# Cross-attention on one core: the step order of the last tiles, the PSUM banks of the score columns, and the operands of the vector norm

## The chip, the cores and the metric

The kernel runs on one core of a Trainium2 chip. The engines of the core are TensorE (PE, matmuls; PEld is its weight load), VectorE (DVE), ScalarE (ACT), GpSimd (POOL) and SyncE (SP, which issues all DMAs here). Each works through its own instructions in order. The working memory is SBUF; matmuls write to PSUM, which has eight banks of 128 partitions by 512 floats. The metric is device time in microseconds (us) of one execution.

## The reference

Four sequences of 2048 rows of x (512 wide) attend to four contexts of 77 rows (384 wide), everything in float32. Cut to what is computed:

```python
text_p  = x @ W_text + b_text
audio_p = ctx @ W_audio + b_audio
Q = layer_norm(text_p, g1, beta1)
K = layer_norm(audio_p, g2, beta2)
alpha = softmax(Q @ K.T / sqrt(512))
h = (alpha @ audio_p) @ W_out + b_out
out = layer_norm(h + x, g_out, beta_out)
```

## The kernel before, in words

The projection of x is never formed. The kernel computes, once for each sequence, a matrix M with which x gives the unscaled scores directly, and vw, the context's values already multiplied by W_out. The variance of a projected row, which the first layer norm needs, is a quadratic form of x; U holds its (upper triangular) matrix in four column chunks. M and U stand side by side in `mu` (two buffers, one for each parity of the sequence); U's last chunk stands in `ub`.

The 8192 rows of x are 64 tiles of 128 rows. Four tiles are a group, which is one load of x (`load_x`, five buffers) and four of a second, spread copy xq (`spread_x`, two buffers). The steps of a tile have one-letter names in the code:

- x (`turn`, L378): DVE turns the tile's xq into xt.
- p and P (`begin_project`, `end_project`, L427 and L435): PE multiplies xt by mu, chunk 3 and 2 in p, chunk 1 and 0 in P, into a bank y; the columns of U's last chunk go to another bank, yl. That is five matmuls a tile, and the profile shows two instructions for each float32 matmul.
- s and t (`score`, `score_rest`): DVE takes the 80 score columns out of y (L462) and sums the products of U's columns with x (L451), for y in s and for yl in t.
- r, c, e for a batch of tiles: POOL computes the row scale by a power (L477, L187), DVE scales the scores and takes the maximum (L484, L487), ACT takes the exponentials (L494).
- w and W (`turn_weights`, L506, L507): PE turns the weights of two tiles, ACT copies them to et.
- a (`apply`, L514): PE multiplies et by vw into a bank h. i, z (L520, L527): DVE inverts the sums and forms z = h/sum + x. q, d (L535, L543, L544, L187): ACT sums the squares, ACT and POOL make the mean and the inverse deviation of the second norm.
- The second norm goes one of two ways. o, y, m: DVE makes a shift (L566), ACT normalizes z (L571), POOL multiplies by g_out and adds beta_out (L575, L576). v (`norm_on_vector`, L558, L559): DVE does it in two instructions. In either way the tile is then stored (L551).

PSUM has eight banks: two for y, two for h, one for each of yl0 and yl1, prep and gain. yl of tile n is in bank yl0 or yl1 by the parity of n, and the turned weights (`et_ps`) use the other one. From slot 20 on, copies of the rows w (used by L484) and of g_out (`kept[1]`, in bank gain) stand in PSUM. The vector norm writes its intermediate zc into the y bank scored last, reads g_out from bank gain (from SBUF before slot 20), and beta_out from SBUF.

The order is the order in which the code is written: `in_program_order` ties each instruction to the one before on its engine. Two pieces of code issue the steps. For slots n = 0 to 39 a loop (L711 to L731) issues, with n the tile being projected: p of n, s and t of n-1, P of n, the norm of n-12, x of n+2, z of n-7, a of n-6, and at fixed slots of every four the batch's steps. The vector norm there is that of every fourth tile, and stands ahead of x and z of its slot. A list written out by hand (L734 to L761) holds all steps from tile 40 on; the batches there are of two tiles from tile 48 on and of one tile for 62 and 63 (`LAST`, L385). Copies of the next sequence's M into mu (L676, POOL) stand at slots 15, 20 and 36. In the list 13 tiles go the way of v (33, 36, 42, 43, 47, 50, 52, 55, 56, 58, 60, 62, 63), in the loop seven (3, 7, ... 27).

Of the kernel before, what the change touches and what calls it, by code (L numbers as in the profile page):

```python
# [29 lines left out]
P = 128  # L30
# [18 lines left out]
def tile_xattn(  # L49
# [40 lines left out]
    def bank(tag, name):  # L90
        return (ps2 if tag in ("h", "y") else ps1).tile([P, 4, P], F32, tag=tag, name=name)

# [85 lines left out]
    four = [flat(bank(tag, f"w_ps_{tag}_{i}")) for i, tag in enumerate(("y", "y", "yl0", "yl1"))]  # L178
# [22 lines left out]
    def prepare(batches, last_columns):  # L201
# [19 lines left out]
        def turned_rows(rows, src, tag):  # L221

            n = rows.stop - rows.start
            pt = bank("prep" if in_slots or tag == "vat" else "gain", f"{tag}_ps_{b0}_{rows.start}")
            for k in range(src.shape[1] // P):
                nc.tensor.transpose(
                    pt[:, k, :n], src[:n, k * P : (k + 1) * P], ident[:n, :n]
                )
            return pt[:, : src.shape[1] // P, :n]
# [155 lines left out]
    LAST = [2, 2, 2, 2, 2, 2, 2, 1, 1]  # L385
    batches, start = [], 0
    for size in [T] * ((NT - sum(LAST)) // T) + LAST:
        batches.append(range(start, start + size))
        start += size
    batch_of = {n: tiles for tiles in batches for n in tiles}  # L390

    ys, state, kept, scored_y = {}, {}, [], []
    begun = [-1]
# [25 lines left out]


    def project_chunks(n, ks):
        mub = made[groups[n // T][0]][0]
        xt = turned[n]
        y, b = ys[n]
        for k in ks:
            cols = slice(0, SQ + min(k + 1, LAST_K) * R)
            nc.tensor.matmul(  # L427
                parts(y[:, : Q * AQ])[:, :, cols],
                lhsT=xt[:, k, :],
                rhs=mub[:, k, :, cols],  # L430
                start=(k == LAST_K),
                stop=(k == 0),
            )
            if k == LAST_K:
                nc.tensor.matmul(  # L435
                    b, lhsT=xt[:, k, :], rhs=ub.rearrange("p q i -> p (q i)"), start=True, stop=True
                )

    def begin_project(n):

        begun[0] = n
        slot_begins(n)
        ys[n] = flat(bank("y", f"y_{n}")), flat(bank(f"yl{n % 2}", f"yl_{n}"))[:, :P]
        project_chunks(n, (3, 2))

    def end_project(n):
        project_chunks(n, (1, 0))
        del turned[n]

    def sum_of_products(y, x, first, to):  # L450
        nc.vector.tensor_tensor_reduce(  # L451
            out=y, in0=y, in1=x, scale=1.0, scalar=first, op0=ALU.mult, op1=ALU.add, accum_out=to
        )

    def score(n):

        i, t = divmod(n, T)
        scored_y[:] = ys[n][:1]
        y = parts(ys[n][0][:, : Q * AQ])
# [3 lines left out]
        xp = parts(xs[i][:, t, :])[:, :, : LAST_K * R]  # L463
        sum_of_products(y[:, :, SQ:], xp, e[:, S : S + 1], s.sa[:, c])

    def score_rest(n):

        i, t = divmod(n, T)
        s, c = of(n)
        yl = parts(ys.pop(n)[1])  # L470
        sum_of_products(yl, parts(xs[i][:, t, :])[:, :, LAST_K * R :], s.sa[:, c], s.ss[:, c])

    def row_scale(f):

        s = state[f]
# [4 lines left out]
    def scale_scores(f):  # L480
        s = state[f]
# [7 lines left out]
    def exponential(f):  # L489
        s = state[f]  # L490
# [5 lines left out]
    def turn_weights(f, a=0):  # L496


        s = state[f]
        z = a + min(s.m, 2) if s.m == T else s.m  # L500
        if a == 0:
            s.et = soft.tile([S, T, P], F32, name=f"et_{f}", tag="et")

        pe = bank(f"yl{(begun[0] + 1) % 2}", f"et_ps_{f}_{a}")
# [13 lines left out]
    def invert(f):  # L518
        s = state[f]
        nc.vector.reciprocal(s.inv[:, : s.m], s.inv[:, : s.m])  # L520

    def residual(n):

        i, t = divmod(n, T)
        s, c = of(n)
        z = s.z[n] = zs.tile([P, H], F32, name=f"z_{n}", tag="z")
# [12 lines left out]
    def deviations(f):  # L539

        s = state[f]
# [11 lines left out]
    def norm_on_vector(n):  # L553
        s, c = of(n)
        z = s.z[n]

        zc = scored_y[0]
        nc.vector.scalar_tensor_tensor(zc, z, s.nm[:, c], kept[1] if kept else go, ALU.add, ALU.mult)  # L558
        nc.vector.scalar_tensor_tensor(z, zc, s.ro[:, c], beo, ALU.mult, ALU.add)  # L559
        store(n)  # L560

    def norm_shift(f):

        s = state[f]
# [3 lines left out]
    def norm_on_scalar(n):  # L568
        s, c = of(n)
        z = s.z[n]  # L570
        nc.scalar.activation(z, z, AF.Identity, bias=s.no[:, c], scale=s.ro[:, c])  # L571

    def norm_on_gpsimd(n):
        z = of(n)[0].z[n]
        nc.gpsimd.tensor_tensor(z, z, go, ALU.mult)  # L575
        nc.gpsimd.tensor_tensor(z, z, beo, ALU.add)  # L576
        store(n)

# [76 lines left out]
    M_MOVED = 4  # L655
    KEPT = 20
    later_steps = prepare(list(range(1, B)), 0)

    def keep():

        kept.append(bank("prep", "w_ps"))
        for b in range(B):
            nc.scalar.copy(kept[0][:, b, :S], made[b][1][:, 1, :S])
        kept.append(flat(bank("gain", "gain_ps")))
        nc.scalar.copy(kept[1], go)

    def slot_begins(n):

        i, t = divmod(n, T)
        b, g = groups[i]  # L670
        if t == 0:
            load_x(i + 2)
        if t == 2:
            spread_x(i + 2)
        if b + 1 < B and n % (NG * T) == (M_MOVED if b else NG * T - 1):
            nc.gpsimd.tensor_copy(  # L676
                mu[(b + 1) % 2][:, :, :, :SQ], later[b + 1].rearrange("p k (q m) -> p k q m", q=Q)
            )

    do = dict(  # L680
        x=turn,
        p=begin_project,
        P=end_project,
        s=score,
        t=score_rest,
        r=row_scale,
        c=scale_scores,
        e=exponential,
        w=turn_weights,
        W=lambda f: turn_weights(f, T // 2),  # L690
        i=invert,
        a=apply,
        z=residual,
        q=squares,
        d=deviations,
        o=norm_shift,
        y=norm_on_scalar,
        m=norm_on_gpsimd,
        v=norm_on_vector,
    )  # L700

    def run(steps, n):

        for step, back in steps:
            if n - back >= 0:
                do[step](n - back)

    for n in range(40):  # L711
        t = n % T
        run([("p", 0), ("s", 1), ("t", 1), ("P", 0)], n)
        on_vector = t == T - 1
        if not on_vector:
            run([("o", 12)] * (t == 0) + [("y", 12)], n)
        if t == 0:
            run([("r", 4)], n)
        run([("v" if on_vector else "m", 12)], n)
        if n == KEPT:  # L720
            keep()
        else:
            next(steps if n < 2 else later_steps, None)
        run([("x", -2)], n)
        run([("i", 7)] * (t == 3) + [("z", 7)], n)
        if t == 0:
            run([("c", 4)], n)
        run([("a", 6)], n)
        run({1: [("w", 5)], 2: [("W", 6)]}.get(t, []), n)
        run([("q", 7)], n)  # L730
        run({0: [("e", 4)], 2: [("d", 10)]}.get(t, []), n)  # L731


    for step in """  # L734
        o28
        p40 s39 z33 y28 y29 a34 t39 a35 r36 z34 P40 c36
        p41 m29 s40 y31 x42 t40 P41 m31
        p42 z35 y30 P42 q33 q34 s41 q35 e36 t41 d32 w36 m28 x43
        p43 s42 P43 o32 t42 a36 y35 i36 v33 x44 y32 a37 s43
        p44 x46 m30 t43 W36 P44 r40 z36 z37 a39 m32 a38 x45 c40 s44 y34 z39  # L740
        p45 P45 t44 q37 z38 e40 x47
        p46 q36 s45 x48 q39 P46 m35 t45 q38 s46 w40 d36 i40 o36 m34 y38
        p47 P47 t46 W40 v36 a40 y37 s47 z40 a42 t47 a43 z42 x50 x49 a41 z41 z43 q42 q40 m38 y39
        p48 q41 r44 P48 c44 q43 m37 s48
        p49 d40 t48 e44 x51 w44 v43 P49 W44 a45 m39 a47 o40 s49
        p50 y41 i44 x52 t49 m41 z45 P50 z47 a46 q45 v42 z46 a44 y40 s50 q47 z44 x53 t50 r48 q46 m40
        p51 P51 c48 s51
        p52 t51 q44 d44 e48 o44 y45 x54 r50 i48 m45 P52 w48
        p53 P53 s52 a48 y46 c50 t52 e50 a49 x55 v47 m46 s53 y44 i50 z48 t53 w50
        p54 P54 x56 q48 z49 s54 a51 a50 z51 r52  # L750
        p55 z50 q49 m44 t54 c52 q51 x57 P55 q50 d48 d50 o48 s55 e52 i52 o50
        p56 t55 v50 y48 w52 P56 s56 a52 m48 r54 a53 y49
        p57 z52 m49 t56 y51 z53 c54 q52 P57 x58 q53 e54 w54
        p58 x59 a55 d52 s57 t57 o52 P58 v52 r56 i54 c56 y53 x60
        p59 s58 z55 t58 P59 e56 a54 w56 s59 i56 z54
        p60 t59 m53 P60 x61 m51 a57 r58 a56 q54 q55 x62 c58 s60 d54 o54 z57 e58 y54
        p61 z56 m54 t60 v55 q57 w58 P61 i58 q56 a59 d56 a58 s61 x63
        p62 t61 o56 y57 P62 z58 z59 r60 m57
        p63 q59 c60 s62 P63 e60 v56 q58 t62 s63 i60 d58 o58 w60 t63 a60 r62 c62 z60 a61 r63 y59 e62 w62 i62
        c63 e63 a62 q60 z61 i63 w63 z62 v58 a63 q61 q62 m59 z63 d60 o60 d62 v60 v62 q63 y61 d63 m61 v63  # L760
    """.split():  # L761
        do[step[0]](int(step[1:]))
# [36 lines left out]
```

## Time and profile before

| | us |
|---|---|
| median of 3 runs | 309.1 (308.82 to 309.45) |
| the profiled execution | 309.45 |
| its span, first to last instruction | 306.6 |
| 64 residuals z on DVE (L527) | 46.7 busy, 734 ns each |
| 64 transposes xt on DVE (L378) | 44.7 busy, 703 ns each |
| 20 vector norms on DVE, L558 and L559 | 15.3 and 15.0 busy |
| 44 norms on POOL, L575 and L576 | 56.0 and 56.2 busy, 1272 and 1277 ns each |
| 44 norms on ACT (L571) | 35.1 busy, 808 ns each |
| 64 second stages on PE (L514), 2 instructions each | 63.9 busy, 596 ns each |

The page has a line for each engine with its busy time, share of the span and number of instructions. The 40 slices show the busy share in equal parts of the span, in tenths. Engines work side by side, so busy times do not add up to the span; the chain of waits tells which of them the end waited for. Groups of instructions have mean durations; the timeline has single ones with their start.

### The profile page before, as it was taken

How to read it: one execution, taken by the hardware profiler on the slowest of the kernel's cores; microseconds unless marked ns; L12 is line 12 of the kernel's file. 1: busy time of each engine (PE TensorE's matmuls, PEld its weight loads, DVE VectorE, ACT ScalarE, POOL GpSimd, SP SyncE). 2: the span in 40 equal slices, each digit the busy share in tenths (PEclk: the TensorE clock that was granted, in tenths of full speed). 3: DMA queues.
4: the chain of work that ended last, by engine and by line, in shares of the span. 5: the costliest groups of instructions: out<-in, count | busy, mean ns of one | idle time of the engine just before them, and what ended most of it. 6: DMA issues, size and time to landing. Idle time of an engine off the chain costs nothing.

```text
span 306.6 us, 4110 instructions
## 1 busy us (share of the span) xinstructions
PE 291.1 (95%) x1096; PEld 177.2 (58%) x1096; DVE 241.3 (79%) x742; ACT 135.8 (44%) x398; POOL 163.2 (53%) x195
## 2 busy tenths in 40 slices
PE   8899999999999999989999999999999999999950
PEld 8568565566777556555555655655555565565520
DVE  3643368877855776998998989888989998999985
ACT  3241011063532243463654536374737656527471
POOL 0010002010552346656867585779888787876774
PEclk9999999999999999999999999999999999999995
DMA  7998792907418616819596969688896979320214
GB/s 237 234 368 260 200 214 97 250 20 138 138 38 168 205 54 157 245 70 253 197 271 175 279 152 285 146 266 166 297 225 207 237 243 202 112 101 34 105 53 186
DMA packets 54356, 55.85 MB, mean 182 GB/s; under 512 B 2531, under 2 KB 35619, under 8 KB 54333
## 3 DMA queue, kind: packets, MB, share of 16 engines
q1 hardware_dynamic: 54333, 55.59, 66.8%
q8 instruction: 8, 0.13, 0.2%
q14 instruction: 15, 0.12, 0.1%
HBM read 38.49 MB, written 16.78 MB: 180 GB/s over the span
## 4 chain that ended last, share of the span: by engine, by line
PE 84%; DVE 7%; DMA 4%; issue 1%; ACT 1%; SPq 1%; POOL 0%; ACTq 0%; DVEq 0%
PE y L427 46%; PE h L514 16%; PE yl L435 4%; PE vw_ps L235 3%; PE m_ps L305 3%; PE va_ps L235 3%; PE et_ps L506 2%; DMA wa<-in_L_xattn_W_audio_dram 2%; PE w_ps_yl L623 2%; DMA xq<-in_x_dram 2%; PE uw_ps L328 2%; DVE y L451 1%; DVE y L558 1%; DVE z L559 1%; PE w_ps_y L623 1%
## 5 line engine op out<-in xcount | busy, mean ns | idle before, releaser
L427 PE MATMUL y<-mu,xt 128*128 128x464 f32 (+2 forms) x512 | 179.0, 473 | 0.0
L427 PEld LDWEIGHTS y<-mu,xt 128*128 128x128 f32 x512 | 89.7, 190 | 49.4 <-issue 34.2
L575 POOL TENSOR_TENSOR z<-z,go 128x512 f32<-128x512 f32 x44 | 56.0, 1272 | 26.6 <-ACT z L571 26.4
L514 PE MATMUL h<-vw,et 77*128 77x512 f32 x128 | 63.9, 596 | 1.3 <-ACT et L507 1.2
L535 ACT ACTIVATE sqj<-z,sz 128x512 f32<-128x512 f32 x64 | 46.2, 722 | 38.1 <-DVE z L527 34.5
L576 POOL TENSOR_TENSOR z<-z,beo 128x512 f32<-128x512 f32 x44 | 56.2, 1277 | 3.4
L527 DVE SCALAR_TENSOR_TENSOR z<-h,inv,x 128x512 f32<-128x512 f32 x64 | 46.7, 734 | 4.8 <-PE h L514 3.4
L378 DVE STREAM_TRANSPOSE xt<-xq 128x512 f32<-128x512 f32 x64 | 44.7, 703 | 0.0
L451 DVE CUSTOM_DVE_ANT_1 y<-y,x,e 128x384 f32<-128x384 f32 x64 | 40.1, 626 | 2.3
L507 ACT COPY et<-et_ps 77x256 f32<-77x256 f32 (+1 forms) x33 | 11.9, 362 | 64.4 <-PE et_ps L506 64.4
L571 ACT ACTIVATE z<-z,no,ro 128x512 f32<-128x512 f32 x44 | 35.1, 808 | 10.9 <-DVE no L566 10.8
L435 PEld LDWEIGHTS yl<-ub,xt 128*128 128x128 f32 x128 | 23.5, 188 | 26.4 <-issue 13.0
L477 POOL TENSOR_SCALAR rs<-ss 128x4 f32<-128x4 f32 (+2 forms) x21 | 4.8, 227 | 51.2 <-DVE ss L451 31.2
L462 DVE TENSOR_TENSOR e<-y,uw 128x80 f32<-128x80 f32 x64 | 15.1, 236 | 20.6 <-PE y L427 20.4
L514 PEld LDWEIGHTS h<-vw,et 77*128 77x128 f32 x128 | 23.0, 190 | 11.7 <-issue 5.9
L494 ACT ACTIVATE e<-e,mx 128x77 f32<-128x77 f32 x64 | 22.3, 352 | 15.3 <-DVE mx L487 15.1
L451 DVE CUSTOM_DVE_ANT_1 yl<-yl,x,sa 128x128 f32<-128x128 f32 x64 | 22.7, 354 | 3.4
L435 PE MATMUL yl<-ub,xt 128*128 128x128 f32 x128 | 24.7, 274 | 0.0
L187 POOL TENSOR_TENSOR rs<-rs,mhalf 128x4 f32<-128x4 f32 (+2 forms) x21 | 18.6, 887 | 1.7
L187 POOL TENSOR_TENSOR ro<-ro,mhalf 128x4 f32<-128x4 f32 (+2 forms) x21 | 18.3, 871 | 1.8
L506 PEld LDWEIGHTS et_ps<-ident,e 128*77 128x77 f32 x64 | 9.1, 147 | 15.8 <-issue 10.3
L544 POOL TENSOR_SCALAR ro<-sq 128x4 f32<-128x4 f32 (+2 forms) x21 | 4.1, 194 | 22.9 <-ACT sqj L535 14.6
(99 smaller groups left out, 274.6 us busy)
## 6 DMA issues: line engine op xcount, KB each, us to landing
xq<-in_x_dram SPq DMA_DIRECT2D x64, 256.0 KB, 5.2
x<-in_x_dram SPq DMA_DIRECT2D x16, 1024.0 KB, 7.3
out_dram<-z SPq DMA_DIRECT2D x64, 256.0 KB, 2.3
wc<-in_L_xattn_W_text_dram SPq DMA_DIRECT2D x2, 512.0 KB, 4.4
wo<-in_L_xattn_W_out_dram SPq DMA_DIRECT2D x1, 1024.0 KB
wa<-in_L_xattn_W_audio_dram SPq DMA_DIRECT2D x1, 768.0 KB
ba<-in_L_xattn_b_audio_dram SPq DMA_DIRECT2D x1, 256.0 KB
bc<-in_L_xattn_b_text_dram SPq DMA_DIRECT2D x1, 256.0 KB
```

The lines of the kernel that those rows point to most:

```text
L187: nc.gpsimd.tensor_tensor(dst, v, mhalf[: v.shape[0], : v.shape[1]], ALU.pow)
L378: nc.vector.transpose(xt.rearrange("p k (a j) -> p a k j", j=R), xq[i][:, t].rearrange("p a (k i) -> p a k i", i=R),)
L427: nc.tensor.matmul(parts(y[:, : Q * AQ])[:, :, cols], lhsT=xt[:, k, :], rhs=mub[:, k, :, cols], start=(k == LAST_K), stop=(k == 0),)
L435: nc.tensor.matmul(b, lhsT=xt[:, k, :], rhs=ub.rearrange("p q i -> p (q i)"), start=True, stop=True)
L451: nc.vector.tensor_tensor_reduce(out=y, in0=y, in1=x, scale=1.0, scalar=first, op0=ALU.mult, op1=ALU.add, accum_out=to)
L494: nc.scalar.activation(e, e, AF.Exp, bias=s.mx[:, c], accum_out=s.inv[:, c])
L514: nc.tensor.matmul(s.h[n], lhsT=s.et[:, n - s.tiles[0], :], rhs=s.vw, start=True, stop=True)
L527: nc.vector.scalar_tensor_tensor(z, s.h.pop(n), s.inv[:, c], xs[i][:, t, :], ALU.mult, ALU.add, accum_out=s.sz[:, c])
L535: nc.scalar.activation(junk, s.z[n], AF.Square, bias=s.sz[:, c], scale=-float(H), accum_out=s.sq[:, c])
L571: nc.scalar.activation(z, z, AF.Identity, bias=s.no[:, c], scale=s.ro[:, c])
L575: nc.gpsimd.tensor_tensor(z, z, go, ALU.mult)
L576: nc.gpsimd.tensor_tensor(z, z, beo, ALU.add)
```

## The change

The projection is no longer split into p and P: `project(n, due)` issues all five matmuls, and for a short batch the turned weights after the first two. y and yl have two banks each, the turned weights have one bank, et, of their own (`bank("et", ...)`), and bank gain is gone. The vector norm works in place, z to z, and its factors are `gains`: go and beo in SBUF, until at slot 64 both are copied to PSUM banks that y and yl no longer need (`keep_gains`). s and t are one step.

The loop now runs to the end, with queues: tiles whose weights are turned wait in `to_apply`, those with their deviations made in `to_norm`, and those for DVE in `on_vector`. How many are taken in a slot is a rule for the first 52 to 56 slots and a table (`APPLIES`, `NORMS`, `VECTOR_NORMS`) after. Batches are of four tiles up to tile 55, then of 3, 2, 2 and 1. The vector norm comes last in its slot, after x, z, c and e. Copies of M stand at slots 15, 31 and 47. Up to slot 39 all other steps stand in the slots where they stood. 13 tiles from slot 40 on still go the way of v (31, 35, 39, 43, 47, 51, 55, 57, 58, 59, 61, 62, 63).

From the program, slots 56 to 69 of the new order, in the letters above (p is the whole projection, s holds t; c56*3 is the scaling of the three tiles from 56 on):

```
56: p56 s55 o44 y44 y45 r52 m44 m45 x58 i48 z48 c52*4 a49 q48 e52
57: p57 s56 y46 m46 x59 z49 a50 w52 q49 v47
58: p58 s57 x60 z50 a51 W52 q50
59: p59 s58 r56 x61 z51 c56*3 a52 a53 q51 e56 d48
60: p60 w56*3 s59 o48 y48 m48 x62 i52 z52 z53 a54 a55 q52 q53
61: p61 s60 y49 y50 r59 m49 m50 x63 z54 z55 c59*2 a56 q54 q55 e59 d52
62: p62 w59*2 s61 i56 z56 a57 a58 q56 v51
63: p63 s62 o52 y52 r61 m52 z57 z58 c61*2 a59 a60 q57 q58 e61 d56
64: w61*2 s63 y53 y54 r63 m53 m54 KEEP i59 z59 z60 c63*1 a61 a62 q59 q60 e63 d59 v55
65: w63*1 o56 y56 m56 i61 z61 z62 q61 q62 d61 v57
66: a63 v58 v59
67: o59 y60 m60 i63 z63 q63 d63
68: v61
69: v62 v63
```

The core of the diff:

```diff
-        return (ps2 if tag in ("h", "y") else ps1).tile([P, 4, P], F32, tag=tag, name=name)
+        return (ps2 if tag in ("h", "y", "yl") else ps1).tile([P, 4, P], F32, tag=tag, name=name)
...
-    LAST = [2, 2, 2, 2, 2, 2, 2, 1, 1]
+    LAST = [3, 2, 2, 1]
+    END = NT - sum(LAST)
+    APPLIES = {52: 0, 53: 0, 54: 2, 59: 2, 60: 2, 62: 2, 63: 2, 65: 0, 67: 1, 68: 0, 69: 1}
+    NORMS = [2, 3, 0, 2, 1, 2, 1, 1, 3, 3, 1, 1, 1, 2, 1, 1, 1, 2, 2]
+    BY_VECTOR = (57, 58, 59, 61, 62, 63)
+    VECTOR_NORMS = {56: 3, 57: 2, 58: 0, 59: 3, 62: 3, 64: 3, 65: 1, 66: 3}
...
-    def begin_project(n):
-        begun[0] = n
-        slot_begins(n)
-        ys[n] = flat(bank("y", f"y_{n}")), flat(bank(f"yl{n % 2}", f"yl_{n}"))[:, :P]
-        project_chunks(n, (3, 2))
-    def end_project(n):
-        project_chunks(n, (1, 0))
-        del turned[n]
+    def project(n, due):
+        y = flat(bank("y", f"y_{n}"))
+        b = flat(bank("yl", f"yl_{n}"))[:, :P]
+        for k in reversed(range(ND)):
...
+            if k == LAST_K:
...
+                for s in due:
+                    turn_weights(s, 0, s.m)
...
-        pe = bank(f"yl{(begun[0] + 1) % 2}", f"et_ps_{f}_{a}")
+        pe = bank("et", f"et_ps_{f}_{a}")
...
-        zc = scored_y[0]
-        nc.vector.scalar_tensor_tensor(zc, z, s.nm[:, c], kept[1] if kept else go, ALU.add, ALU.mult)
-        nc.vector.scalar_tensor_tensor(z, zc, s.ro[:, c], beo, ALU.mult, ALU.add)
+        gain, bias = gains
+        nc.vector.scalar_tensor_tensor(z, z, s.nm[:, c], gain, ALU.add, ALU.mult)
+        nc.vector.scalar_tensor_tensor(z, z, s.ro[:, c], bias, ALU.mult, ALU.add)
...
+    def keep_gains():
+        for i, (tag, v) in enumerate((("y", go), ("yl", beo))):
+            gains[i] = flat(bank(tag, f"gain_ps_{i}"))
+            nc.scalar.copy(gains[i], v)
...
-    M_MOVED = 4
-    KEPT = 20
+    M_MOVED = 3
+    W_KEPT = 20
...
-    for n in range(40):
-        t = n % T
-        run([("p", 0), ("s", 1), ("t", 1), ("P", 0)], n)
...
+    while n < NT or applied or to_apply or to_norm or on_vector or n < NT + 3:
...
+            project(n, ended(n - 2, True))
...
+        for q in on_vector[: VECTOR_NORMS.get(n, 1 + (n >= NT))]:
+            norm_on_vector(q)
+            on_vector.remove(q)
+        n += 1
```

The norm's two instructions are L559 and L560 in the new file, the small shift L567, POOL's two L577 and L578.

## The prediction

> **What bounds the kernel now.** I read the page's busy shares and 40 slices first. TensorE (PE) is busy 95% and every slice before the last two reads 8 or 9, so until tile 63 is projected the time is PE's sum.
>
> ```profile
> PE 291.1 (95%) x1096; PEld 177.2 (58%) x1096; DVE 241.3 (79%) x742; ACT 135.8 (44%) x398; POOL 163.2 (53%) x195
> PE   8899999999999999989999999999999999999950
> DVE  3643368877855776998998989888989998999985
> ```
>
> VectorE (DVE) reaches 8 and 9 too from slice 17 on, so it is the second engine. Next came the busy time by stretch: one batch of four tiles in the steady loop, and the stretch after tile 63 (columns: stretch, length, then busy time of PE, weight load, DVE, ACT, POOL).
>
> ```profile
> 155.25:169.93 14.68, 14.68 (x54) 8.68 (x53) 12.99 (x41) 7.61 (x23) 10.09 (x10) 1.00 0.87 228
> 199.28:290.57 91.29, 90.39 (x316) 52.40 (x315) 83.88 (x267) 52.59 (x151) 73.52 (x82) 1.00 0.66 184
> 290.57:303.25 12.68, 4.87 (x12) 1.77 (x12) 11.16 (x32) 6.59 (x20) 9.00 (x14) 0.85 0.27 104
> ```
>
> In the steady batch PE has no idle time and DVE has 1.69 us in 14.68. 199.28 is the first matmul of tile 40, 290.57 the end of the last of tile 63. After that PE is nearly empty and DVE is busy 11.16 of 12.68: the end of the kernel is a queue on DVE, followed by 3.35 us (303.25 to 306.60) of last store. So span = end of tile 63 on PE + what DVE still has to do then + 3.35.
>
> The chain of waits agrees with that: PE pieces to 288, then vector norms (L558, L559) at the end. The timeline then showed what a DVE instruction costs when both tensors come from SBUF while GpSimd (POOL) runs one of its 128x512 products (start, length, engine).
>
> ```profile
> 120.70 1.27 POOL L576 TENSOR_TENSOR z<-z,beo 128x512 f32<-128x512 f32 x1
> 121.56 0.97 DVE L558 SCALAR_TENSOR_TENSOR y<-z,nm,go 128x512 f32<-128x512 f32 x1
> ...
> 127.70 1.27 POOL L575 TENSOR_TENSOR z<-z,go 128x512 f32<-128x512 f32 x1
> 127.76 2.95 DVE L484 SCALAR_TENSOR_TENSOR e<-e,rs,uw 128x77 f32<-128x77 f32 x4 [0.19 <-POOL rs L187]
> 129.05 1.35 POOL L576 TENSOR_TENSOR z<-z,beo 128x512 f32<-128x512 f32 x1
> 132.69 0.41 PE L506 MATMUL et_ps<-ident,e 128*77 128x128 f32 x2 [0.78 <-DVE ss L451]
> ...
> 259.68 0.70 POOL L187 TENSOR_TENSOR ro<-ro,mhalf 128x2 f32<-128x2 f32 x1
> 259.99 0.12 DVE L566 TENSOR_TENSOR no<-nm,ro 128x2 f32<-128x2 f32 x1
> 261.06 1.27 POOL L575 TENSOR_TENSOR z<-z,go 128x512 f32<-128x512 f32 x1 [0.68 <-ACT z L571]
> 261.24 1.10 DVE L566 TENSOR_TENSOR no<-nm,ro 128x2 f32<-128x2 f32 x1
> ```
>
> L566 takes 0.12 us beside the small power op L187 but 1.10 beside L575, ending at 262.34 where L575 ends at 262.33. The four L484 take 2.95 us instead of 0.97 (the same four at 111.16). At 121.56 the 0.97 is a wait to 121.97 and 0.56 of work. With one operand in PSUM (gain_ps) L558 is 0.72 to 0.76 us whatever POOL does. The line at 132.69 is PE waiting 0.78 us in tile 21's slot, because the turned weights share a bank with yl and wait for the score.
>
> **The change part by part.** Units on DVE, from start to start: score of a tile 1.36 (155.00 to 156.38; 1.27 at best), transpose xt 0.63, residual z 0.72, reciprocal 0.23, no 0.08, scaling a batch of four 1.34 (157.99 to 159.32), of two 0.76 (245.15 to 245.91), of three about 1.05 and of one about 0.5 (between those), vector norm of today 1.46 (152.02 to 153.48).
>
> (1) Matmuls. Both kernels have five a tile; instruction counts per tile are equal, so this part is 0 on PE.
>
> (2) A bank of its own for the turned weights: takes away the 0.78 us at 131.9. What is late next there is the exponentials (131.25 plus two of 0.35, the accumulator reads and a handover, about 132.1), so 0.2 to 0.3 of it stays: gain 0.5, bounds 0 and 0.8.
>
> (3) Vector norms of the loop (seven up to slot 39, six in slots 43 to 62) lose both PSUM operands: L559 and L560 read z with go, z with beo, all in SBUF. Free of POOL each is 0.56, with a handover of 0.1 some 1.2 a norm, 0.25 less than now. Beside POOL's products each half waits for the running product and POOL's next one slips in between: (0 to 1.27) + 0.56 + 1.35 + 0.56 = 2.5 to 3.7, middle 3.1. Which one holds depends on the slot. In the steady loop the norm moves behind xt and z of its slot, to about 153.6 and 168.2 in the two batches shown by the timeline; POOL's products there end at 152.87 and 167.12, then comes L187 until 154.25 and 168.87, then nothing until 156.60 and 171. L187 does not hold L566 up in the rows above, so the price is 1.2 and PE, which has DVE's 1.69 us as cover, gains nothing. Without that cover it would be 1.65 us a batch (3.1 - 1.46) against 1.69. The Trainium skill, "SBUF — State Buffer", section "SBUF: two separate sides", says that a VectorE op with two SBUF inputs and a GpSimd op that reads SBUF exclude one another for a whole instruction. It would make L187 a blocker as well, against the 0.12 us row; by it some 0.65 us a batch more lies in the slack, and the sum stays.
>
> (4) The copies of mu to the other buffer move from slots 20 and 36 to 31 and 47, last slot before their use. POOL reaches them behind L187 (about 168.9 in the batch whose next tile starts at 169.93) and needs 0.45: 0 if nothing interferes, at most 0.3 each when a norm on DVE holds it: I take 0.
>
> (5) Order from tile 40 on. In the loop DMAs keep their order; from slot 40 on loads of x and xq stand up to two stores earlier or later on SP's queue, and xt is made two slots ahead, as in the loop, where it never waits. I take 0. The PE sum: a tile is 0.78 + 0.22 + 1.70 = 2.70 (chain of waits), an h 0.86, a pair of turned weights 0.22. Before the end of tile 63 the new order has 24 tiles, 25 h (34 to 58) and 25 turned tiles: 64.8 + 21.5 + 2.75 = 89.05, from 199.28 to 288.33, and 287.8 with the gain of (2). Today it is 290.57, with 26 h and 0.90 us of idle time. Here the change is 2.8 us ahead.
>
> (6) What DVE has left. With tiles 56 to 63 PE needs 31.2 us (8 x 2.70, 10 h, 5 turned). DVE in the same slots: 4.36, 5.81, 2.71, 3.76, 3.74, 4.19, 5.41, 3.64 by the units, 33.6, plus the last score 1.36. Slots 57 and 62 hold a vector norm (tiles 47 and 51) next to two elementwise tiles on POOL (45, 46; 49, 50), so there I take 3.1. DVE may start 0.86 early. It ends the last score 2.2 to 2.9 us after PE's tile 63; stepping the slots through one by one I get 2.2 (1.36 when nothing collides). Then in program order: z59, z60 1.67; scaling of 63 0.5; v55 1.46; z61, z62 1.67; v57, v58, v59 4.4; z63 with its reciprocal 1.03; v61, v62, v63 4.5. Sum 15.2. Two waits belong to it: v55 for go and beo, which ACT copies to PSUM (0.58 each) behind two norms of 0.80: 0.6. And the small L567 of tile 56 behind POOL's product of tile 54: 0 to 1.3, 1.1 by the slots. 287.8 + 2.2 + 15.2 + 1.7 + 3.35 = 310.3. Today that is 306.6, so +3.7. The profiled execution took 309.45 (2.85 beyond its span) and the median of the runs is 309.1; to this I add 3.7: **312.8 us**.
>
> **Rivals.** (A) No collisions: norms 47 and 51 fall into POOL's gaps, v55 and L567 don't wait. 287.8 + 1.36 + 15.2 + 3.35 = 307.7, +1.1 to +1.6 with small waits: 310.2 to 310.9. For it: POOL is busy only 73.52 of 91.29 us in this stretch. Against it: exactly these slots have two tiles on POOL.
>
> (B) The collisions come in the steady loop as well, because POOL lags into the norm. Then 1.65 us a batch meets some 1.2 us of true slack (1.69 less the small handovers); 0.45 a batch over eight batches, 3.6 us: about 316. Against it: the POOL rows leave 0.7 us of margin.
>
> (C) Faster: the bank of its own and the closer packing count, and the tail stays 16.03 us as now: 287.8 + 16.03 = 303.8, 306.3 as a median. It decides if DVE's list after tile 63 takes no more than 15.4 us, that is today's 12.68 plus the 2.8 us won. By the units the list is 1.36 + 15.2 = 16.6 before any wait, and nothing in it can run before tile 63's y. So it needs instructions 7% shorter than today's rows.
>
> (D) The words of the change (five matmuls in place of eight) don't describe it: no matmul goes away, only order and banks. This is so by the counts, and no forecast here rests on it.
>
> **How the numbers follow.** Forecast 0.64 (311.0 to 314.6), A 0.20, B 0.08, C 0.05, no change 0.03. Under 0.2% (0.6 us, the spread of the three runs, 308.82 to 309.45) I count as no change. A lies above that bound, so slower is 0.92. The range is from A's low end to between forecast and B: 310.2 to 315.4.
>
> **What would show it.** Tile 63's last matmul at 287 to 289, earlier than 290.57, and 20 to 23 us from there to the end, with five z, seven vector norms and little idle time on DVE. L559 and L560 near 0.56 us in the loop's fourth slots, and over 1 us in the two norms near 263 to 267 and 282 to 285. The PE wait near 132 shortened to under 0.4. It is wrong if tile 63 ends later than 290 (then PE waits for something in (3) to (5)), or if DVE idles more than 3 us in the tail.

## The result and the profile after

| | before | after |
|---|---|---|
| median of 4 runs, us | 308.96 (308.67 to 309.45) | 311.22 (310.76 to 311.34) |
| ratio, 95% interval | | 1.0069 [1.0051, 1.0086] |
| span of the profiled execution, us | 306.6 | 309.4 |
| its time, us | 309.45 | 311.17 |
| end of tile 63 on PE, us | 290.57 | 287.89 |
| end of the last vector norm on DVE, us | 303.25 | 305.96 |

The changed kernel is slower by 0.7%, some 2.3 us in the medians. The spans differ by more, 2.8 us. What lies outside the span (time less span) is not a constant: it went from 1.73 to 2.99 us over the runs of all kernels here, and the profiled execution of before, with 2.85, is near its upper end.

The busy shares and two rows of the 40 slices of the kernel after:

```profile
PE 292.3 (94%) x1096; PEld 179.3 (58%) x1096; DVE 244.8 (79%) x733; ACT 135.2 (44%) x395; POOL 162.7 (53%) x183
PE   8999999999999999999999999999999999999730
DVE  3543378786855677999998988989898989999895
```

PE's row now falls off earlier (7, 3, 0 at the end, where before had 9, 5, 0): PE is done sooner, and DVE has more to do behind it. The busy time by stretch of the kernel after says how much (stretch, length, then PE, weight load, DVE, ACT, POOL, and PE's granted clock): the same steady batch as before; from just ahead of tile 40's first matmul (198.12) to the end of tile 63; the tail, which is all that follows until DVE's last norm ends; the last store.

```profile
155.25:169.93 14.68, 14.68 (x54) 8.73 (x53) 13.00 (x42) 7.59 (x22) 10.48 (x11) 1.00 0.88 227
198.00:287.89 89.89, 89.88 (x317) 53.03 (x316) 82.46 (x255) 48.19 (x138) 64.91 (x66) 1.00 0.62 173
287.89:305.96 18.07, 6.46 (x13) 2.08 (x12) 16.25 (x37) 10.30 (x30) 16.01 (x20) 0.67 0.36 136
305.96:309.40 3.44, 0.00 (x0) 0.00 (x0) 0.00 (x0) 0.00 (x0) 0.00 (x0) 0.50 0.53 208
```

The steady batch is as long as before, 14.68 us. Tile 63 ends 2.68 us earlier, the tail is 18.07 us instead of 12.68, the store 0.09 longer: -2.68 + 5.39 + 0.09 = +2.8, the difference of the spans. In the tail DVE is busy 16.25 us (11.16 before) and POOL 16.01 (9.00 before): both queues have become long, not DVE's alone. PE's granted clock is lower in the tail too (0.67, before 0.85), and its last two instructions for h took 2.08 us where the last two before took 1.12. Nobody waited for them: they end at 297.56, and DVE comes to the z of tile 63 at 300.74.

Ahead of tile 63 the turned weights' own bank takes a wait away. In tile 21's slot PE's timeline shows the turned weights with no wait, where before they had 0.78 us:

```profile
131.85 0.38 PE L510 MATMUL et_ps<-ident,e 128*77 128x128 f32 x2
```

Below, a tile's place on PE is given by the start of its matmul into yl, one row a tile in the timeline. (The title calls yl's banks those of the score columns; yl holds the columns of U's last chunk, and the 80 score columns stand in y.)

The vector norms have three prices. A half is one of the norm's two instructions. The timeline of the kernel after shows norm 47, beside two tiles on POOL, and one norm of the steady loop; the two groups by form are the norms whose factors stand in PSUM (from slot 64 on).

```profile
260.72 1.28 POOL L577 TENSOR_TENSOR z<-z,go 128x512 f32<-128x512 f32 x1
262.07 1.82 DVE L559 SCALAR_TENSOR_TENSOR z<-z,nm,go 128x512 f32<-128x512 f32 x1
262.08 1.26 POOL L578 TENSOR_TENSOR z<-z,beo 128x512 f32<-128x512 f32 x1
263.30 1.72 POOL L577 TENSOR_TENSOR z<-z,go 128x512 f32<-128x512 f32 x1
263.93 1.65 DVE L560 SCALAR_TENSOR_TENSOR z<-z,ro,beo 128x512 f32<-128x512 f32 x1
265.10 1.60 POOL L578 TENSOR_TENSOR z<-z,beo 128x512 f32<-128x512 f32 x1
```

```profile
152.29 1.02 POOL L187 TENSOR_TENSOR ro<-ro,mhalf 128x4 f32<-128x4 f32 x1
152.46 0.75 DVE L559 SCALAR_TENSOR_TENSOR z<-z,nm,go 128x512 f32<-128x512 f32 x1
153.24 0.75 DVE L560 SCALAR_TENSOR_TENSOR z<-z,ro,beo 128x512 f32<-128x512 f32 x1
```

```profile
L560 DVE SCALAR_TENSOR_TENSOR z<-z,ro,gain_ps 128x512 f32<-128x512 f32 x7 | 5.2, 747 | 0.5
L559 DVE SCALAR_TENSOR_TENSOR z<-z,nm,gain_ps 128x512 f32<-128x512 f32 x7 | 5.2, 742 | 0.0
```

Norm 47 runs from 262.07 to the next instruction at 265.50, 3.43 us; each half waits for the product of POOL that starts with it or ahead of it (262.08 + 1.26 and 263.30 + 1.72 are their ends). Free of POOL a half from SBUF takes 0.75, as long as one with its factor in PSUM.

### The profile page after: what moved, and what is told of

The parts are those of the page before. It is cut to its first block, busy times and chain, and to the rows that moved or that the text cites. A ratio compares the mean times of both kernels' runs of the same rounds, so it can differ in the third digit from the quotient of the medians.

```text
span 309.4 us, 4098 instructions
## 1 busy us (share of the span) xinstructions
PE 292.3 (94%) x1096; PEld 179.3 (58%) x1096; DVE 244.8 (79%) x733; ACT 135.2 (44%) x395; POOL 162.7 (53%) x183
## 5 line engine op out<-in xcount | busy, mean ns | idle before, releaser
L577 POOL TENSOR_TENSOR z<-z,go 128x512 f32<-128x512 f32 x44 | 56.3, 1280 | 30.6 <-ACT z L575 30.6
L518 PE MATMUL h<-vw,et 77*128 77x512 f32 x128 | 66.0, 603 | 0.9 <-ACT et L511 0.9
L578 POOL TENSOR_TENSOR z<-z,beo 128x512 f32<-128x512 f32 x44 | 56.8, 1291 | 3.5
L529 DVE SCALAR_TENSOR_TENSOR z<-h,inv,x 128x512 f32<-128x512 f32 x64 | 46.1, 727 | 3.3 <-PE h L518 1.6
L511 ACT COPY et<-et_ps 77x256 f32<-77x256 f32 (+2 forms) x32 | 11.7, 366 | 63.1 <-PE et_ps L510 63.1
L456 PEld LDWEIGHTS yl<-ub,xt 128*128 128x128 f32 x128 | 24.2, 189 | 25.6 <-issue 20.8
L485 POOL TENSOR_SCALAR rs<-ss 128x4 f32<-128x4 f32 (+3 forms) x18 | 4.1, 228 | 51.5 <-DVE ss L476 30.2
L187 POOL TENSOR_TENSOR ro<-ro,mhalf 128x4 f32<-128x4 f32 (+3 forms) x18 | 18.2, 1008 | 1.5
L187 POOL TENSOR_TENSOR rs<-rs,mhalf 128x4 f32<-128x4 f32 (+3 forms) x18 | 17.4, 967 | 1.5
L546 POOL TENSOR_SCALAR ro<-sq 128x4 f32<-128x4 f32 (+3 forms) x18 | 4.4, 247 | 22.0 <-ACT sqj L537 12.8
```

The costliest lines, as they stand in the source:

```text
L187: nc.gpsimd.tensor_tensor(dst, v, mhalf[: v.shape[0], : v.shape[1]], ALU.pow)
L456: nc.tensor.matmul(b, lhsT=xt[:, k, :], rhs=ub.rearrange("p q i -> p (q i)"), start=True, stop=True)
L518: nc.tensor.matmul(s.h[n], lhsT=s.et[:, n - s.tiles[0], :], rhs=s.vw, start=True, stop=True)
L529: nc.vector.scalar_tensor_tensor(z, s.h.pop(n), s.inv[:, c], xs[i][:, t, :], ALU.mult, ALU.add, accum_out=s.sz[:, c])
```

## The experiments

Each ran beside runs of the kernel before on the same chip. Ratios are to these; differences in us are of medians on that chip.

### What each part is worth

**The new order with the old banks and the old norm.** The kernel after, with yl0, yl1 and bank gain put back, the turned weights in the other yl bank, and the norm through zc with g_out from bank gain:

```diff
-        b = flat(bank("yl", f"yl_{n}"))[:, :P]
+        b = flat(bank(f"yl{n % 2}", f"yl_{n}"))[:, :P]
...
-        pe = bank("et", f"et_ps_{f}_{a}")
+        pe = bank(f"yl{(begun[0] + 1) % 2}", f"et_ps_{f}_{a}")
...
-        nc.vector.scalar_tensor_tensor(z, z, s.nm[:, c], gain, ALU.add, ALU.mult)
-        nc.vector.scalar_tensor_tensor(z, z, s.ro[:, c], bias, ALU.mult, ALU.add)
+        zc = scored_y[0]
+        nc.vector.scalar_tensor_tensor(zc, z, s.nm[:, c], kept[1] if kept else go, ALU.add, ALU.mult)
+        nc.vector.scalar_tensor_tensor(z, zc, s.ro[:, c], beo, ALU.mult, ALU.add)
...
-        if n == NT:
-            keep_gains()
```

> The changed kernel's order and batches with the banks and the norm of the kernel before: turned weights share the yl banks, g_out in PSUM from slot 20, the norm's intermediate in the y bank, no copies at slot 64. Theory (the order of the last tiles makes the loss, through what DVE has left after tile 63): +1.2 to +2.6 us against the kernel before, the 0.78 us wait of PE near 132 back, norms of tiles 47 and 51 at 1.5 us. Rival (operands and banks make it): within 0.6 us of the kernel before.

Measured: 314.43 against 308.76, ratio 1.0188 [1.0168, 1.0209], +5.7 us. That is well above the range of the theory (+1.2 to +2.6). The timeline shows the shared bank's wait in tile 21's slot, half as long as before, a weight load that waits for the norm's second half (L563 here), and the end of tile 63 (288.94 + 1.86):

```profile
132.37 0.41 PE L513 MATMUL et_ps<-ident,e 128*77 128x128 f32 x2 [0.38 <-DVE ss L479]
...
140.39 0.30 PEld L450 LDWEIGHTS y<-mu,xt 128*128 128x128 f32 x2 [0.97 <-DVE z L563]
...
288.94 1.86 PE L450 MATMUL y<-mu,xt 128*128 128x464 f32 x6
```

Tile 63 ends at 290.80, 2.91 us later than in the kernel after and where before had it, so the new order gains nothing on PE by itself. It brings the long tail (21.1 us from there to the end of the span), and the new banks and operands together give 3.4 us of the 5.7 back, 2.5 by the spans (311.9 against 309.4). The loss was larger than I expected of any theory, since I had costed the banks as a matter of one wait. The view of PE's waits has another, of the weight loads of y (sum in us, times, longest):

```profile
PEld y L450 <- DVE z L563: 5.6, 8, 1.0
```

In this kernel the norm's intermediate lies in the y bank scored last, which the next tile needs, and the norm stands last in its slot. By the starts of yl PE falls 0.7 us behind the kernel after at tiles 22 and 23, where the turned weights wait. It falls behind by 0.16 to 0.41 us at each of tiles 20, 24, 28, 36, 40, 44 and 52, which come behind a vector norm and such a wait; that is 1.4 us in sum. At tile 58, behind norm 47, it is 0.74 us, where the view names another releaser. So the shared bank is the smaller part of PE's loss here, and the larger one goes with the norm through y. This is read from the trace; bank and operands were not tried one by one.

**The in-place norm in the old order.** The kernel before, with nothing but the norm's operands changed:

```diff
-        zc = scored_y[0]
-        nc.vector.scalar_tensor_tensor(zc, z, s.nm[:, c], kept[1] if kept else go, ALU.add, ALU.mult)
-        nc.vector.scalar_tensor_tensor(z, zc, s.ro[:, c], beo, ALU.mult, ALU.add)
+        nc.vector.scalar_tensor_tensor(z, z, s.nm[:, c], go, ALU.add, ALU.mult)
+        nc.vector.scalar_tensor_tensor(z, z, s.ro[:, c], beo, ALU.mult, ALU.add)
```

> The kernel before with one edit: the vector norm works in place, z with go and z with beo, both from SBUF, to the end. Theory (exclusion): the 13 norms from slot 40 on stand where POOL is busy and cost 0 to 2 us more each, DVE is the tail's engine, so the end is 4 to 14 us later than the kernel before; the seven of the loop stay near 1.5 us where POOL is idle. Rival (operands cost nothing): within 0.6 us of the kernel before.

Measured: 319.13 against 308.76, ratio 1.0337 [1.0302, 1.0372], +10.4 us. The groups of the two lines (count, busy, mean ns):

```profile
L557 DVE SCALAR_TENSOR_TENSOR z<-z,nm,go 128x512 f32<-128x512 f32 x20 | 26.0, 1302 | 0.0
L558 DVE SCALAR_TENSOR_TENSOR z<-z,ro,beo 128x512 f32<-128x512 f32 x20 | 21.1, 1056 | 0.9
```

47.1 us for the 20 norms, against 30.3 before and 33.3 in the kernel after (11.9 + 11.0 + 5.2 + 5.2). In the old order the two instructions cost 16.8 us of DVE more than before; in the new one, with the norm last in its slot and the tail's factors in PSUM, 3.0 more. The next run, the new order without the copies to PSUM, has 38.4 us. So of the 13.8 us between the orders 8.7 come from where the norms stand and 5.1 from the copies. The loop's norms, expected near 1.5 us, missed that: five of the seven took about 2.5 us (1.70 and 0.75 at 137.41), because ahead of x and z they start beside a product of POOL.

**The tail's factors left in SBUF.** The kernel after without the call of `keep_gains`:

```diff
-        if n == NT:
-            keep_gains()
```

> The changed kernel without the copies of g_out and beta_out to PSUM at slot 64: the seven last vector norms read both operands from SBUF while POOL is busy 16.0 of 18.1 us. Theory (a two-SBUF-operand DVE instruction and a POOL product exclude one another): each of the seven norms takes 2.5 to 3.5 us instead of 1.5, POOL's products are stretched as well, the end is 5 to 12 us later than the changed kernel. Rival (the place of the operands is worth only the difference in read time, none in the loop where both forms take 0.75): within 1 us of the changed kernel.

Measured: 316.74 against 308.76, ratio 1.0256 [1.0237, 1.0274], +8.0 us, where the kernel after has +2.3: the two copies are worth 5.7 us. The timeline shows the two engines holding one another up:

```profile
299.06 1.37 POOL L577 TENSOR_TENSOR z<-z,go 128x512 f32<-128x512 f32 x1
299.22 1.75 DVE L559 SCALAR_TENSOR_TENSOR z<-z,nm,go 128x512 f32<-128x512 f32 x1
300.50 1.59 POOL L578 TENSOR_TENSOR z<-z,beo 128x512 f32<-128x512 f32 x1
301.00 1.63 DVE L560 SCALAR_TENSOR_TENSOR z<-z,ro,beo 128x512 f32<-128x512 f32 x1
```

**The loop's half alone.** The kernel before, with the turned weights in a bank of their own until slot 40, the in-place norm last in its slot until then, and the copy of g_out made after slot 39; the list from tile 40 on is the old one:

```diff
-        pe = bank(f"yl{(begun[0] + 1) % 2}", f"et_ps_{f}_{a}")
+        pe = bank("gain" if begun[0] < 40 else f"yl{(begun[0] + 1) % 2}", f"et_ps_{f}_{a}")
...
-        run([("v" if on_vector else "m", 12)], n)
+        if not on_vector:
+            run([("m", 12)], n)
...
         run({0: [("e", 4)], 2: [("d", 10)]}.get(t, []), n)
+        if on_vector:
+            run([("v", 12)], n)
+    keep_gain()
```

> The kernel before with the changed kernel's loop up to slot 39 (turned weights in a bank of their own, the vector norm last in its slot, in place, with operands from SBUF) and its own hand-written list and banks from tile 40 on (g_out copied to PSUM at slot 40). Theory (the own bank gains about 1 us by tile 40, in the loop the norm meets an idle POOL, and the loss is all in the order of the last tiles): 0.7 to 1.1 us earlier than the kernel before, 2.9 to 3.4 us earlier than the changed kernel. Rival (the gain is given back later, because DVE is the engine of the last 90 us): within 0.3 us of the kernel before.

Measured: 307.57 against 308.58, ratio 0.9973 [0.9957, 0.9989], -1.0 us. The first tile's yl starts 0.31 us later than before (30.71 against 30.40), tile 40's 0.74 sooner (199.16 against 199.90; 198.90 after). So the loop's half of the change is a gain, and the loss is all in the part from tile 40 on. The gain comes at one place: before, PE loses some 1.0 us to this kernel at tiles 22 and 23 and keeps step with it at all others up to tile 40.

### The collisions of the loop's norms

**Norm 47 one slot later**, out of the slot in which POOL works on tiles 45 and 46:

```diff
-    VECTOR_NORMS = {56: 3, 57: 2, 58: 0, 59: 3, 62: 3, 64: 3, 65: 1, 66: 3}
+    VECTOR_NORMS = {56: 3, 57: 0, 58: 1, 59: 3, 62: 3, 64: 3, 65: 1, 66: 3}
```

> The changed kernel with the vector norm of tile 47 one slot later (slot 58 instead of 57), where POOL is idle. In the changed kernel that norm took 1.82 + 1.65 us beside POOL's products. Theory (DVE's delay before tile 63 was absorbed, since it began the last score 0.03 us after PE's tile 63): the norm takes about 1.5 us, tile 63 on PE and the end stay within 0.3 us of the changed kernel, +1.7 to +2.6 us against the kernel before. Rival (collisions in slots 57 and 62 reach the end): 1.5 to 2 us less than the changed kernel, about +0.5 against the kernel before.

Measured: 310.72 against 308.76, ratio 1.0065 [1.0049, 1.0080]; the interval is nearly that of the kernel after. The norm took 2.22 us instead of 3.43 (264.86 to 267.08), not the expected 1.5. PE started tile 63's yl at 285.12 instead of 285.81; 0.10 us of that is there from the first tile on. The last half norm on DVE starts sooner by as much, at 304.62 instead of 305.21, and the span was 308.8, 0.6 less:

```profile
304.62 0.75 DVE L560 SCALAR_TENSOR_TENSOR z<-z,ro,gain_ps 128x512 f32<-128x512 f32 x1
```

The theory had this collision absorbed ahead of tile 63. It was not: some 0.6 us of it reaches tile 63 on PE, and 0.5 the end. That is still far from the rival's 1.5 to 2 us. Against before the medians give +2.0 us, where the kernel after has +2.3. The rival, that this collision carries a large part of the loss, falls. Norm 51's collision was not tried.

### What the tail is bound by

The forecast read the tail as DVE's list. Three kernels leave a step of some 1.5 to 2.6 us out of it: on DVE, on POOL, and on both. These kernels lack that step for tile 55 or 54, so their rows of the result are not the reference's.

**On DVE:** the vector norm of tile 55 is left out.

```diff
 def norm_on_vector(n):
+        if n == 55:
+            store(n)
+            return
```

> The changed kernel with the vector norm of tile 55 left out (tile 55 is stored as z, so its rows are not the reference's); nothing else moves. That norm is 1.50 us of DVE in the list after tile 63. Theory (the end is DVE's list): the end comes 1.3 to 1.6 us earlier than in the changed kernel, some +0.6 to +1.0 us against the kernel before. Rival (POOL's queue, busy 16.0 of the 18.1 us after tile 63, sets the end through the inverse deviation of tile 63, which stands behind tile 60's products): at most 0.5 us earlier.

Measured: 311.32 against 308.58, ratio 1.0092 [1.0079, 1.0105]: no gain. The shares of the chain of waits, and two vector norms of the timeline (L562 and L563 are the norm's lines here):

```profile
POOL 6%; DVE 2%; issue 0%; POOLq 0%
```

```profile
301.84 0.75 DVE L563 SCALAR_TENSOR_TENSOR z<-z,ro,gain_ps 128x512 f32<-128x512 f32 x1 [0.85 <-POOL ro L187]
...
305.34 0.75 DVE L563 SCALAR_TENSOR_TENSOR z<-z,ro,gain_ps 128x512 f32<-128x512 f32 x1 [0.66 <-POOL ro L187]
```

DVE is free 1.5 us sooner and spends it waiting for the last deviations, which POOL makes behind its products. The theory that DVE's list alone sets the end falls.

**On POOL:** the two products of tile 54 are left out.

```diff
-        nc.gpsimd.tensor_tensor(z, z, go, ALU.mult)
-        nc.gpsimd.tensor_tensor(z, z, beo, ALU.add)
+        if n != 54:
+            nc.gpsimd.tensor_tensor(z, z, go, ALU.mult)
+            nc.gpsimd.tensor_tensor(z, z, beo, ALU.add)
```

> The changed kernel without POOL's two products for tile 54 (its rows lack the gain and bias); 2.57 us of POOL go away in the stretch after tile 63. Theory (the end is DVE's list): only the wait of the small L567 behind that product (0.4 us) and small handovers go, 0.2 to 0.7 us earlier than the changed kernel. Rival (POOL's queue sets the end): 1.5 to 2.6 us earlier, below the kernel before.

Measured: 311.02 against 308.58, ratio 1.0088 [1.0073, 1.0103]: no gain either. POOL now waits for its next tile (L578 is the first product here), and DVE's list ends at 305.86 instead of 305.96:

```profile
301.45 1.27 POOL L578 TENSOR_TENSOR z<-z,go 128x512 f32<-128x512 f32 x1 [1.64 <-ACT z L575]
```

```profile
305.11 0.75 DVE L560 SCALAR_TENSOR_TENSOR z<-z,ro,gain_ps 128x512 f32<-128x512 f32 x1
```

**On both:** the two edits together.

> The changed kernel with both cuts at once: no vector norm for tile 55 and no POOL products for tile 54 (the rows of both tiles are not the reference's). Either cut alone moved nothing, and with either one DVE's list or POOL's queue still ended within 0.2 us of where it ended before. Theory (after tile 63 both queues are full and equally long, so the end is the later of the two): with both shorter (DVE by 1.5, POOL by 2.6) the end comes 1.2 to 2.0 us earlier than the changed kernel. Rival (something common to both sets the end, such as the stores or the chain of tile 63 through PE and ACT): again within 0.4 us of the changed kernel.

Measured: 309.86 against 308.30, ratio 1.0044 [1.0031, 1.0058], +1.6 us, span 307.8. The last half norm on DVE starts 1.56 us sooner than in the kernel after (305.21 there):

```profile
303.65 0.75 DVE L563 SCALAR_TENSOR_TENSOR z<-z,ro,gain_ps 128x512 f32<-128x512 f32 x1
```

Either step alone brought nothing; both together brought 1.6 us of the profiled span. The middle of all spans says 1.1 (308.1, where the kernel after has 309.2), and the differences to before 0.7 (+1.6 against +2.3). The interval lies clear of those of either step alone, but it overlaps a little with that of the kernel after. So the direction is shown, and the size lies between 0.7 and 1.6 us. That is what two queues of equal length beside one another show: DVE's and POOL's both end where the kernel ends.

### Towards a faster kernel

The small collisions that the forecast's rows show stand in the kernel before as well. **The row copy read late:** before, the batch that is scaled in slot 20 reads w from SBUF, though its copy to PSUM is made then; the operand is chosen when the batch is created. The kernel before, with the choice made at the instruction:

```diff
-            self.w = kept[0][:, groups[f // T][0], :S] if kept else self.uw[:, 1, :S]
...
+        w = kept[0][:, groups[f // T][0], :S] if kept else s.uw[:, 1, :S]
         for q in range(s.m):
...
-                e, e, s.rs[:, q : q + 1], s.w, ALU.mult, ALU.add
+                e, e, s.rs[:, q : q + 1], w, ALU.mult, ALU.add
```

> The kernel before with one edit: the scaling of the scores reads the PSUM copy of the rows w as soon as that copy exists, so the batch of slot 20 uses it (it read SBUF there, and four L484 took 2.95 us beside POOL's products). Theory (that collision makes PE's 0.78 us wait near 132 in the kernel before, and up to 0.4 more over the next two tiles): the wait goes, PE reaches tile 40 0.7 to 1.1 us earlier, and the end comes 0.5 to 1.1 us earlier than the kernel before. Rival (the shared bank alone makes it): within 0.3 us of the kernel before.

Measured: 307.44 against 308.58, ratio 0.9965 [0.9952, 0.9978]. The four instructions that took 2.95 us beside POOL's products:

```profile
128.08 0.91 DVE L484 SCALAR_TENSOR_TENSOR e<-e,rs,w_ps 128x77 f32<-128x77 f32 x4 [0.59 <-ACT w_ps L663]
```

That is 1.1 us less. PE's wait at 132 is gone with it, and tile 63's yl starts at 287.29 instead of 288.49. The wait that the change cures with a bank came, in this slot, from one collision. The kernel after still has the collision (2.96 us at 127.43) and only hides it.

**With one small shift moved as well:** step o50 (L566), which stands at the end of slot 55 behind a product of POOL, goes behind t55:

```diff
-        p55 z50 q49 m44 t54 c52 q51 x57 P55 q50 d48 d50 o48 s55 e52 i52 o50
-        p56 t55 v50 y48 w52 P56 s56 a52 m48 r54 a53 y49
+        p55 z50 q49 m44 t54 c52 q51 x57 P55 q50 d48 d50 o48 s55 e52 i52
+        p56 t55 o50 v50 y48 w52 P56 s56 a52 m48 r54 a53 y49
```

> The kernel before with the PSUM copy of the rows w read as soon as it exists, and the small L566 of tiles 50 and 51 moved behind the second half of the score of tile 55 (it took 1.10 us beside POOL's product and PE waited 0.72 us). Theory (each wait removed ahead of tile 63 is time won): 0.5 to 0.8 us earlier than with the first edit alone, 1.6 to 2.0 us earlier than the kernel before. Rival (DVE, which is full in this stretch, gives it back): no better than the first edit alone, 0.8 to 1.2 us earlier than the kernel before.

Measured: 307.12 against 308.30, ratio 0.9957 [0.9939, 0.9974]; tile 57's yl starts at 264.23 instead of 265.28 in the run without the move, tile 63's at 286.55 instead of 287.29; 0.17 us of both is there from the first tile on. The time, 1.2 us under before, is in the rival's range. The spans (304.3 to 305.1, against 305.3 to 305.8 without the move, on another chip) and PE show the move; in the time the intervals overlap, so there it is not settled.

**The loop's half of the change and the shift moved** (the edits of the fourth and the last diff above, no late read):

> The changed kernel's loop and banks up to slot 39, the old list from tile 40 on, and the small L566 of tiles 50 and 51 moved behind the second half of the score of tile 55. Theory: 0.5 to 0.8 us earlier than without the move, 1.4 to 1.8 us earlier than the kernel before. Rival: 0.7 to 1.1 us earlier than the kernel before, as without it.

Measured: 306.61 (305.97 to 307.15) against 308.30, ratio 0.9933 [0.9912, 0.9954]. This is the fastest kernel here, 1.7 us under before by the medians, where the change is 2.3 over it. It keeps the change's loop and drops its order of the last tiles. Its interval just clears that of the loop without the move (0.9954 against 0.9957). All three versions of this part are faster than before; their order among themselves the intervals leave open.

## Why the prediction was right, and where it was not

The direction held, and the time is in the range. The medians gave +2.3 us and the spans +2.8, where the sum gave +3.7.

**Tile 63 on PE** (steps 1, 2 and 5): 287.8 forecast, 287.89 measured. That the two agree so closely is luck, because two errors cancel. The share given to step 2 was too small: the own bank took away the 0.78 us wholly, not 0.5, and by tile 40 PE is 1.0 us ahead (199.90 to 198.90). The sum of step 5 was too small by about as much: from tile 40's first matmul to the end of tile 63 PE took 89.77 us (198.12 to 287.89), where the sum has 89.05 and starts 0.16 late (199.28 is the end of the matmul ahead; tile 40 begins at 199.12). The unit prices hold where nothing waits. But PE was taken as free of DVE, and norm 47's collision reached it. In the kernel after, a weight load for h waits there for a residual z of DVE (L529), which reads an earlier h out of its bank:

```profile
270.69 0.30 PEld L518 LDWEIGHTS h<-vw,et 77*128 77x128 f32 x2 [0.73 <-DVE z L529]
```

From tile 59's yl to tile 61's PE took 9.75 us (267.86 to 277.61); with norm 47 one slot later it took 9.16. And step 5's win does not stand without the new banks and operands: with the old ones the new order ends tile 63 at 290.80, no sooner than before. The steps were added as if they were independent.

**The norms from SBUF** (step 3): free of POOL a half takes 0.75, not 0.56. I had read 0.56 off a wait that I let end with POOL's product. If a half needs its 0.75 once POOL has let go, POOL lets go some 0.2 us before its recorded end (262.07 + 1.82 - 0.75 = 263.14, where L578 ends at 263.34). So a free norm costs 1.45, as much as before, and nothing was to be won there. In the steady loop it falls free of POOL's products, as forecast, and PE lost nothing; rival B is out. Beside POOL, 3.1 was taken for norms 47 and 51; they took 3.43 and 2.51 (281.94 to 284.45), in the range of 2.5 to 3.7. The Trainium skill, "SBUF — State Buffer", section "SBUF: two separate sides", would have the power op L187 block a norm too. The rows around 152 show L187 (152.29 to 153.31) and L559 at their own lengths side by side: it did not.

**The copies of mu** (step 4): nothing on PE, as forecast; one half of a norm takes 0.91 beside such a copy at 167.91.

**DVE's list** (step 6). This is the step that was mis-sized. "It ends the last score 2.2 to 2.9 us after PE's tile 63" was 1.31. DVE did not lag when tile 63 ended, in spite of norms 47 and 51; it started that score at 287.92, right behind. These 0.9 us are nearly the whole of what the span was missed by (310.3 forecast, 309.4 measured). The trace shows which terms were too long. A score took 1.25 to 1.28 us from start to start, not 1.36; a residual 0.64 to 0.67, not 0.72; and norm 51 took 2.51, not 3.1. The eight slots 56 to 63 took DVE 32.60 us (255.32 to 287.92) instead of 33.6, though norm 47 was dearer than assumed. PE, held up as said above, took 31.93 for them instead of 31.2, which also made DVE's lag smaller. The list behind it held: 15.2 and 1.7 of waits, 16.9, against 16.76 (289.20 to 305.96). Inside it two waits were others than those named. The scaling of tile 63 waited for POOL, and by the time v55's second half began at 293.11 the second gain copy (292.07 + 0.58) was there. L567 waited half of what I gave it, and behind a product of tile 53, not 54: without those of tile 54 it takes 0.58 all the same.

```profile
291.79 0.30 DVE L491 SCALAR_TENSOR_TENSOR e<-e,rs,w_ps 128x77 f32<-128x77 f32 x1 [0.90 <-POOL rs L187]
292.07 0.58 ACT L675 COPY gain_ps<-beo 128x512 f32<-128x512 f32 x1
292.27 0.74 DVE L559 SCALAR_TENSOR_TENSOR z<-z,nm,gain_ps 128x512 f32<-128x512 f32 x1
293.11 0.75 DVE L560 SCALAR_TENSOR_TENSOR z<-z,ro,gain_ps 128x512 f32<-128x512 f32 x1
293.77 0.58 DVE L567 TENSOR_TENSOR no<-nm,ro 128x3 f32<-128x3 f32 x1
```

The forecast also read the tail as DVE's alone. The sum came out near enough, because DVE's list is indeed full; the runs show that POOL's is as full, which the forecast did not look at. Anyone who had shortened DVE's list on the strength of it would have won nothing, as the run without tile 55's norm shows.

**From span to time.** I added the span's difference to the median of before, as if what lies outside the span stayed. The profiled execution of before had 2.85 us there, that of after 1.77; over the runs of before on three other chips the median is 1.8 to 1.9. So the time rose less than the span. Why this part varies, no run shows.

**Rivals.** A (310.2 to 310.9; by its own +1.6 it ends at 310.7) was nearer in time than the forecast and nearer than its mechanism deserved: the collisions did come. C failed where the forecast put its point of decision: the tail needed 18.07 us and not 15.4. D's counts hold: 1096 PE instructions in both.

## What to carry to other kernels

An order that finishes the bounding engine sooner wins only if it does not leave more for the other engines to do after that point. Sum each queue's work behind it, all of them, since shortening one of two equally full queues shows nothing. Put VectorE instructions that read two SBUF tensors where GpSimd has no long products, or give one operand a PSUM copy; the two copies at the end were worth 5.7 us here, and the in-place norm in the old order's slots cost 10 us. Look also at which bank an intermediate occupies, and for how long: the norm through a y bank held PE up once it stood last in its slot. Change a loop and its tail separately: here the loop's half was a gain of about 1 us, hidden under the tail's loss.

## What the hardware showed that was not expected

The exclusion works both ways. POOL's products beside a waiting norm stretch as well: 1.72 and 1.60 us near 263 and 265, where 1.27 is usual. Two streams of dependent instructions then take turns, and both lose.

POOL's small power op does not hold a norm that starts behind it, but is itself held when the norm has started first: L187 on 128x4 took 1.56 us at 138.75, just behind L559 (138.69), and 1.02 at 152.29, just ahead of it.

A half of the norm took 0.75 us with all tensors in SBUF and 0.74 to 0.75 with its factor in PSUM: the copy to PSUM buys no speed, only freedom from POOL.
